# A two-layer graph network on one core: more of layer 0's gathers done as products, and the sums of a batch read later

## The chip, the cores and the metric

The kernel runs on one core of a Trainium2 chip. The metric is the device time in microseconds (us) of one execution; lower is better. Engines are named as in the profile: PE multiplies matrices (PEld loads its weights), DVE is the vector engine, ACT the scalar engine, POOL is GpSimd, SP issues DMAs.

## The reference

There are 12,500 nodes with 48 features and 200,000 edges, sorted by destination. Both layers take the features of each edge's source node, turn them into a message, add the messages up at the destination, and normalise.

```
# layer 0
tmp = concatenate([x[dst], x[src], edge_attr_32], axis=1)
h   = relu(tmp @ W1 + b1)
x1  = layernorm(x + segment_sum(h @ W2 + b2, dst))
# layer 1
m   = relu(x1[src] + edge_attr_48)
out = layernorm((1 + eps) * x1 + x1 + segment_sum(m, dst))
```

## The kernel before

The edges are cut into 391 groups of 512 (`NCHUNK`), each of 4 tiles of 128 edges. One group passes per step `k` of a loop; `run` (L620) calls a list of stages at each step, each with its own distance `d`, so that stage `f` works on group `k - d`. The order in which instructions are written is the order on every engine's queue. The function `lead0` comes last in each step of layer 0.

**Source features by gather.** `gather` (L247) issues one indirect DMA on POOL for one tile: 4 for a group. In layer 0 `fetch0` writes them into the tile `cat` six steps ahead (`AHEAD`). The pool of `cat` has 12 buffers; the last that reads a `cat` is `sum0`, at step g + 4. So the gather of group g waits until PE is through `sum0` of group g - 12, which happens at step g - 8. In layer 1 the tile is `xs`, also with 12 buffers, read by `message1` (`m`, L705).

**Source features by product.** Some groups are not gathered. Their features are made as one-hot matrices times the node table, two groups (8 tiles) to a batch (`products`, L530), as in these steps:

- `place` writes on DVE 8 small comparisons (`which_e`, L485), PE transposes them (L490) into the PSUM tile `which`; in layer 1 ACT makes a `copy` of it (L539).
- `edge_of` (L512) opens three PSUM tiles `ps` with multiplications by zeros; the same function closes them at the end.
- For each of the 98 blocks of 128 nodes (`NT`) a comparison on all 8 tiles gives a one-hot matrix `o` (`select`, L495, DVE; in layer 1 one block in five by `select_by_act`, L500 and L502, ACT), and `multiply` (L507) does 8 matmuls with the block `xp`. The matmuls of one step's blocks are written in the next step.
- `take` (L520) adds the three pieces of each sum on DVE (`made`, L523), one reduction for each of the tiles `ps`.

`products` is a generator; each step calls it once. In layer 0 a call does 2 and 3 blocks by turns (`BPS0 = (2, 3)`), so a batch lasts 40 steps and 8 batches serve the 16 groups 65, 85, ..., 365 (`FIRST0`, `EVERY0`, `NPE0`), from step 20 (`BEGIN0`) to 340. In layer 1 a call does 5 blocks (`BPS`), a batch lasts 20 steps, and 19 batches serve 38 groups: 20, 30, ..., 390. Six groups at the front of layer 1 (`FRONT`) are gathered from the table `front_dram`, with the last segment's rows added by products (`front`).

**Other work of a step in layer 0** on PE: `hidden0` (8 matmuls, L598), `sum0` (8, L613), `turn0` (4 transposes, L587), then the product matmuls. Every 28 groups a segment of nodes ends: `finish0` (`segment_sums`, layer norm, write of `x1_dram`) and, two steps later, `project` of a coming segment. From step `END0` on the finished table is loaded again, two steps for a segment, and split into `xp` for layer 1 (`split`).

**Layer 1** on PE: `sum1` (8 matmuls, L725) into a bank for 12 groups, opened and closed with zeros (L722, L730), then the product matmuls; on DVE `fill1` (`hot`, L695), `message1`, the comparisons; `drain1` and `finish1` at the end of a bank and of a segment. `some_products` calls the generator from group `BEGIN1` on.

Of the kernel before, what the change touches and what calls it, by code (L numbers as in the profile page):

```python
# [32 lines left out]
F32 = mybir.dt.float32  # L33
# [6 lines left out]
P = 128  # L40
# [3 lines left out]
D = 48  # L44
# [4 lines left out]
NT = -(-N // Q)  # L49
# [9 lines left out]
NSEG = NT // NB  # L59
# [10 lines left out]
FIRST = 20  # L70
EVERY = 10
NPE = 38
BEGIN1 = 4
BATCH = 2
BPS = 5
BY_ACT = 2
PIECES = 3

FIRST0 = 65
EVERY0 = 20  # L80
NPE0 = 16
BPS0 = (2, 3)
SPLIT0 = 2
BEGIN0 = 20
END0 = 341

PE_GROUPS0 = [FIRST0 + EVERY0 * i for i in range(NPE0)]
PE_GROUPS = [FIRST + EVERY * i for i in range(NPE)]
# [1 line left out]
assert PE_GROUPS[0] >= FRONT  # L90

assert PE_GROUPS[-1] < NCHUNK and PE_GROUPS0[-1] < NCHUNK
assert 2 * NT < BATCH * EVERY0 * sum(BPS0) and BEGIN0 > SPLIT0 + NSEG + 1
assert CHUNK * N % E == 0
assert NSEG * NB == NT
STEP = CHUNK * N // E
# [64 lines left out]
def windowed(ctx, tc, dram, flag, x, src, dst, e32, e48, w1, b1, w2, b2, eps, out):  # L161
# [15 lines left out]
    psum = layer0.enter_context(tc.tile_pool(name="psum0", bufs=1, space=bass.MemoryType.PSUM))  # L177
# [109 lines left out]
    for op, by, plus, to in (  # L287
# [5 lines left out]
            by, None, op0=op,  # L293
        )
        nc.vector.tensor_scalar(
            bits[:, FRONT + NPE :, :], src_g[:, FIRST0 : PE_GROUPS0[-1] + 1 : EVERY0, :],
            by, None, op0=op,
        )
        nc.vector.tensor_scalar(to, bits, plus, None, op0=ALU.add)
    begin.close()  # L300
    onehots = layer0.enter_context(tc.tile_pool(name="onehots0", bufs=2 * max(BPS0)))
    product = layer0.enter_context(tc.tile_pool(name="product0", bufs=1))
# [126 lines left out]
    def rows_of(table, s):  # L429
        return table[s * SN : (s + 1) * SN, :].rearrange("(t p) d -> p t d", p=Q)  # L430

    def split(t, s):
        for i in range(PIECES):
            piece = xp[:, s * NB : (s + 1) * NB, i, :]
            nc.scalar.activation(piece, t, AF.Copy)
            if i < PIECES - 1:
                rest = node.tile([Q, NB, D], F32, name="rest")
                nc.vector.tensor_tensor(rest, t, piece, op=ALU.subtract)
                t = rest

    def finish0(s):
# [6 lines left out]
        if s < NSEG - 1:  # L448
            nc.scalar.dma_start(rows_of(front_dram, s), x1)
        if last_group(s) >= END0:  # L450
            split(x1, s)
# [15 lines left out]
    def last_group(s):  # L467

        return max(g for g in range(NCHUNK) if low(g) < (s + 1) * SN)
# [7 lines left out]
    PER = 512 // (PIECES * D)  # L477

    def place(first, tiles, name, bufs):

        which = psum.tile([Q, tiles, P], BF16, name=name, bufs=bufs)
        which_e = product.tile([P, tiles, Q], BF16, name="which_e")
        for j in range(tiles):
            i = first + j // TPC
            nc.vector.tensor_scalar(  # L485
                which_e[:, j, :], iota_1, part[:, i, j % TPC : j % TPC + 1],
                block[:, i, j % TPC : j % TPC + 1], op0=ALU.is_equal, op1=ALU.mult,
            )
        for j in range(tiles):
            nc.tensor.transpose(which[:, j, :], which_e[:, j, :], ident16)  # L490
        return which

    def select(which, b):
        o = onehots.tile([Q, which.shape[1], P], BF16, name="o")
        nc.vector.tensor_scalar(o, which, float(b + 1), None, op0=ALU.is_equal)  # L495
        return o

    def select_by_act(copy, b):
        square = product.tile([Q, copy.shape[1], P], BF16, name="square")
        nc.scalar.activation(square, copy, AF.Square, bias=less[:, b : b + 1])  # L500
        o = onehots.tile([Q, copy.shape[1], P], BF16, name="o_act", bufs=2)
        nc.scalar.activation(o, square, AF.Relu, bias=1.0, scale=-1.0)  # L502
        return o

    def multiply(ps, o, b):
        for j in range(o.shape[1]):
            nc.tensor.matmul(  # L507
                ps[j // PER][:, j % PER, :], o[:, j, :], xp[:, b, :, :],
                start=False, stop=False, skip_group_check=True,
            )  # L510

    def edge_of(ps, start):  # L512
        for t in ps:
            n = t.shape[1] * PIECES * D
            nc.tensor.matmul(
                t.rearrange("p k c d -> p (k c d)"), zeros[:, :P], zeros[:, :n],
                start=start, stop=not start,
            )

    def take(ps, first, batch):  # L520
        xs = product.tile([P, batch * TPC, D], F32, name="made", bufs=FRONT // BATCH)
        for k, t in enumerate(ps):
            nc.vector.tensor_reduce(  # L523
                xs[:, k * PER : k * PER + t.shape[1], :], t.rearrange("p k c d -> p k d c"),
                AX.X, ALU.add,
            )
        for i in range(batch):
            made[ahead[first + i]] = xs[:, i * TPC : (i + 1) * TPC, :]

    def products(begin, count, batch, blocks, per_step, by_act, banks, bufs):  # L530


        tiles = batch * TPC
        for first in range(begin, begin + count, batch):
            which = place(first, tiles, banks[0], bufs)
            copy = None
            if by_act is not None:
                copy = product.tile([Q, tiles, P], BF16, name="copy", bufs=2)
                nc.scalar.activation(copy, which, AF.Copy)  # L539
            ps = [  # L540
                psum.tile([P, min(PER, tiles - k), PIECES, D], F32, name=banks[1 + k // PER],
                          bufs=bufs)
                for k in range(0, tiles, PER)
            ]
            edge_of(ps, True)
            last = []
            todo, step = list(blocks), 0
            while todo:
                n = per_step[step % len(per_step)]
                now = [  # L550
                    (b, select_by_act(copy, b) if i == by_act else select(which, b))
                    for i, b in enumerate(todo[:n])
                ]
                todo, step = todo[n:], step + 1
                for c, o in last:
                    multiply(ps, o, c)
                last = now
                yield
            for c, o in last:
                multiply(ps, o, c)  # L560
            edge_of(ps, False)
            take(ps, first, batch)


    cat, h, pt, ph, pa, hot = {}, {}, {}, {}, {}, {}
# [54 lines left out]
    def run(stages, adds, finish, lead):  # L620
# [13 lines left out]

    whole = {}
    work0 = products(
        FRONT + NPE, NPE0, BATCH, range(NT), BPS0, None, ("which", "sums0", "sums1", "sums2"), 1
    )

    def lead0(k):  # L640
# [10 lines left out]
        for s in range(NSEG):  # L651
# [3 lines left out]
            if k == SPLIT0 + s + 2:  # L655
                split(whole.pop(s), s)
            if last_group(s) < END0:
                if k == END0 + 2 * s + 1:
                    whole[s] = seg.tile([Q, NB, D], F32, name="whole", bufs=2)
                    nc.sync.dma_start(whole[s], rows_of(x1_dram, s))  # L660
                if k == END0 + 2 * s + 4:
                    split(whole.pop(s), s)
# [24 lines left out]
    psum = ctx.enter_context(tc.tile_pool(name="psum", bufs=1, space=bass.MemoryType.PSUM))  # L687
# [69 lines left out]
    banks = ("pm", "ph", "ph", "pm")  # L757

    def front():
# [19 lines left out]
        take(*before, BATCH)  # L779

    rest = products(FRONT, NPE, BATCH, range(NT), (BPS,), BY_ACT, banks, 2)

    def some_products(g):
        if g >= BEGIN1:
            next(rest, None)
# [225 lines left out]
```

## Time and profile before

| what | value |
|---|---|
| median of 3 runs | 3701.22 us (3698.91 to 3702.09) |
| the profiled execution, its own time | 3699.33 us |
| its span, first to last instruction | 3697.6 us |
| mean granted clock of PE | 0.885 |
| gathers in layer 0 / front / layer 1 | 1500 / 24 / 1388 |
| first gather; last of layer 0; last of all, ends at | 7.1; 1893.2; 3679.5 us |

Times in the text are from the start of the profiled span. In a line of the timeline the columns are start, duration over all of its instructions, engine, source line, operation, what it writes and reads, its shape, the count, and in brackets the idle time of the engine before it with what ended that. In a table by stretches each engine has its busy time and, in brackets, its instructions; the clock, the DMA share and GB/s follow.

### The profile page before, as it was taken

The numbers are of one execution on the slowest core, as the hardware profiler recorded it, in microseconds if no ns is written. First come the engines' busy times: TensorE is split into PE (matmuls) and PEld (weight loads), VectorE is DVE, ScalarE is ACT, GpSimd is POOL, SyncE is SP. The second block draws the span as 40 slices with busy tenths as digits, with TensorE's granted clock in tenths as the row PEclk, the third lists the DMA queues.
The fourth block names the chain that finished last, engine by engine and source line by source line (L and its number), as shares of the span: only waits on it lengthen the run. The fifth ranks groups of instructions, "written<-read, shape, count | busy, mean of one in ns | idle before, by whom it ended". The sixth has DMA issues, their size and how long they took to land. (4 is left out here: it accounts for less than half of the span.)

```text
span 3697.6 us, 87599 instructions
## 1 busy us (share of the span) xinstructions
PE 3348.4 (91%) x33806; PEld 2968.8 (80%) x33806; DVE 2683.3 (73%) x5415; ACT 1365.6 (37%) x2178; POOL 2774.8 (75%) x2923
## 2 busy tenths in 40 slices
PE   5888998998999899887889999999999999999996
PEld 4887988897888798886768887888888888888884
DVE  4765876676777686674438788788878888888883
ACT  2211211121112121113215555565556555655562
POOL 7777777777777777777776777777777777777776
PEclk8887988898989898897659999999999999999996
DMA  4222222122222212223211122122212221222121
GB/s 94 50 50 44 47 50 52 39 55 47 46 47 53 51 44 49 49 48 68 46 35 37 43 46 46 42 52 46 46 43 46 51 46 37 52 46 51 37 52 35
DMA packets 326421, 177.43 MB, mean 48 GB/s; under 512 B 144384, under 2 KB 325744, under 8 KB 326000
## 3 DMA queue, kind: packets, MB, share of 16 engines
q0 software_dynamic: 93184, 71.75, 11.3%
q1 hardware_dynamic: 203152, 88.86, 9.0%
q10 hardware_dynamic: 29664, 11.16, 1.1%
q8 instruction: 269, 4.41, 0.5%
q14 instruction: 152, 1.25, 0.1%
HBM read 156.51 MB, written 15.03 MB: 46 GB/s over the span
## 5 line engine op out<-in xcount | busy, mean ns | idle before, releaser
L247 POOL DMA_INDIRECT cat<-in_x_dram,src_i x1500 | 1429.2, 953 | 460.8 <-issue 310.3
L247 POOL DMA_INDIRECT xs<-x_dram,src_i x1388 | 1320.0, 951 | 435.9 <-issue 291.1
L507 PEld LDWEIGHTS <-o 128*128 128x128 bf16 x18296 | 1250.4, 102 | 99.4 <-DVE o L495 41.9
L495 DVE TENSOR_SCALAR o<-pm 128x1024 bf16<-128x1024 bf16 x1503 | 942.5, 686 | 62.2 <-ACT copy L539 27.1
L507 PE MATMUL ph<-xp,o 128*128 128x144 bf16 x8976 | 808.8, 231 | 0.0
L602 ACT ACTIVATE h<-ph 128x512 f32<-128x512 f32 x391 | 233.0, 596 | 1110.7 <-PE pa L613 1086.1
L598 PE MATMUL ph<-wcat,cat_t 128*128 128x128 f32 x3128 | 507.4, 313 | 106.4 <-ACT h L602 106.3
L598 PEld LDWEIGHTS ph<-wcat,cat_t 128*128 128x128 f32 x3128 | 448.0, 221 | 127.4 <-ACT h L602 120.8
L725 PE MATMUL pt<-hot,msg 128*48 128x128 f32 x3128 | 447.9, 290 | 56.5 <-ACT msg L711 56.5
L495 DVE TENSOR_SCALAR o<-which 128x1024 bf16<-128x1024 bf16 x784 | 495.3, 680 | 3.1 <-PE which L490 3.0
L507 PE MATMUL sums<-xp,o 128*128 128x144 bf16 x6272 | 488.6, 238 | 0.0
L725 PEld LDWEIGHTS pt<-hot,msg 128*48 128x48 f32 x3128 | 341.0, 129 | 141.4 <-ACT msg L711 63.8
L507 PE MATMUL pm<-xp,o 128*128 128x144 bf16 x2978 | 438.9, 230 | 0.0
L613 PE MATMUL pa<-cat,h 128*128 128x48 f32 x3128 | 431.6, 285 | 5.4 <-DVE pa L606 5.1
L613 PEld LDWEIGHTS pa<-cat,h 128*128 128x128 f32 x3128 | 429.2, 212 | 6.8 <-issue 4.7
L500 ACT ACTIVATE square<-copy,less 128x1024 bf16<-128x1024 bf16 x380 | 430.7, 1133 | 0.7
L502 ACT ACTIVATE o_act<-square 128x1024 bf16<-128x1024 bf16 x380 | 401.6, 1057 | 17.2 <-PE pm L507 5.8
L587 PE MATMUL pt<-ident,cat 128*128 128x128 f32 x1564 | 292.4, 302 | 82.5 <-DMA cat<-in_x_dram,src_i 79.3
L695 DVE TENSOR_TENSOR hot<-pa,rel 128x512 f32<-128x512 f32 x391 | 269.8, 690 | 97.6 <-PE pt L725 96.6
L591 DVE COPY cat_t<-pt 128x512 f32<-128x512 f32 x391 | 266.9, 683 | 72.3 <-PE pt L587 68.9
L711 ACT ACTIVATE msg<-m 128x192 f32<-128x192 f32 x391 | 141.5, 362 | 456.9 <-DVE m L705 408.4
L587 PEld LDWEIGHTS pt<-ident,cat 128*128 128x128 f32 x1564 | 214.7, 171 | 110.2 <-DMA cat<-in_x_dram,src_i 105.7
(118 smaller groups left out, 2412.1 us busy)
## 6 DMA issues: line engine op xcount, KB each, us to landing
e48c<-in_e_dram SPq DMA_DIRECT2D x78, 480.0 KB
e32c<-in_e_dram SPq DMA_DIRECT2D x78, 320.0 KB
cat<-in_x_dram,src_i POOLq DMA_INDIRECT x1500
xs<-x_dram,src_i POOLq DMA_INDIRECT x1388
wcat<-a SPq DMA_DIRECT2D x391, 24.0 KB
a<-a ACTq DMA_DIRECT2D x14, 256.0 KB
a<-a ACTq DMA_DIRECT2D x14, 192.0 KB
x_seg<-in_x_dram SPq DMA_DIRECT2D x14, 168.0 KB
```

The lines of the kernel that those rows point to most:

```text
L247: nc.gpsimd.indirect_dma_start(out=t, out_offset=None, in_=table, in_offset=bass.IndirectOffsetOnAxis(ap=src_i[:, g * TPC + j : g * TPC + ...
L495: nc.vector.tensor_scalar(o, which, float(b + 1), None, op0=ALU.is_equal)
L500: nc.scalar.activation(square, copy, AF.Square, bias=less[:, b : b + 1])
L502: nc.scalar.activation(o, square, AF.Relu, bias=1.0, scale=-1.0)
L507: nc.tensor.matmul(ps[j // PER][:, j % PER, :], o[:, j, :], xp[:, b, :, :], start=False, stop=False, skip_group_check=True,)
L587: nc.tensor.transpose(pt[g][:, j, :], cat[g][:, j, :], ident[:P, :P])
L591: nc.vector.tensor_copy(h[g], pt.pop(g))
L598: nc.tensor.matmul(ph[g][:, j, :], t[:, j, :], wcats[g % NW], start=True, stop=True)
L602: nc.scalar.activation(h[g], ph.pop(g), AF.Relu)
L613: nc.tensor.matmul(pa[g][:, 0, :], t[:, j, :], hot[:, j, :], start=j == 0, stop=j == TPC - 1)
L695: nc.vector.tensor_tensor(o, numbers[:, None, :].to_broadcast([P, TPC, W1]), rel1[:, g, :, None].to_broadcast([P, TPC, W1]), op=ALU.is_equal,)
L725: nc.tensor.matmul(bank[k][:, i * STEP : i * STEP + W1], msg[:, j, :], o[:, j, :], start=False, stop=False, skip_group_check=True,)
```

## The change

Layer 0 makes 20 groups by products instead of 16: 58, 75, ..., 381 (every 17th). A call does 3 blocks at every step, so a batch lasts 33 steps, and ten batches run from step 20 to 350. The splits for layer 1 begin at 352 instead of 341. In layer 1 the products begin one step later.

In `products`, for both layers, `take` of a batch is written later: no longer right after the matmuls that close its sums, but after the next batch's `place`, `copy` and first comparisons. The next batch's `ps` and their opening zeros follow `take`, since they use the same PSUM banks. The last batch's `take` comes at the end.

```diff
-BEGIN1 = 4
+BEGIN1 = 5
...
-FIRST0 = 65
-EVERY0 = 20
-NPE0 = 16
-BPS0 = (2, 3)
+FIRST0 = 58
+EVERY0 = 17
+NPE0 = 20
+BPS0 = (3,)
 SPLIT0 = 2
 BEGIN0 = 20
-END0 = 341
+END0 = 352
...
         tiles = batch * TPC
+        before = None
         for first in range(begin, begin + count, batch):
             which = place(first, tiles, banks[0], bufs)
             copy = None
             if by_act is not None:
                 copy = product.tile([Q, tiles, P], BF16, name="copy", bufs=2)
                 nc.scalar.activation(copy, which, AF.Copy)
-            ps = [
...
-            edge_of(ps, True)
-            last = []
+            ps = last = None
             todo, step = list(blocks), 0
             while todo:
...
                 todo, step = todo[n:], step + 1
-                for c, o in last:
-                    multiply(ps, o, c)
+                if ps is None:
+                    if before:
+                        take(*before)
+                    ps = [
+                        psum.tile([P, min(PER, tiles - k), PIECES, D], F32,
+                                  name=banks[1 + k // PER], bufs=bufs)
+                        for k in range(0, tiles, PER)
+                    ]
+                    edge_of(ps, True)
+                else:
+                    for c, o in last:
+                        multiply(ps, o, c)
                 last = now
                 yield
             for c, o in last:
                 multiply(ps, o, c)
             edge_of(ps, False)
-            take(ps, first, batch)
+            before = ps, first, batch
+        take(*before)
```

More of the change, by code (lines that the diff above doesn't have):

```diff
@@ L92 @@
 assert PE_GROUPS[-1] < NCHUNK and PE_GROUPS0[-1] < NCHUNK
-assert 2 * NT < BATCH * EVERY0 * sum(BPS0) and BEGIN0 > SPLIT0 + NSEG + 1
+assert NT < BATCH * EVERY0 * BPS0[0] and BEGIN0 > SPLIT0 + NSEG + 1
 assert CHUNK * N % E == 0
@@ L539, in products @@
                 nc.scalar.activation(copy, which, AF.Copy)
-            ps = [
[L541 to L544, printed above, removed]
-            edge_of(ps, True)
-            last = []
+            ps = last = None
             todo, step = list(blocks), 0
```

## The prediction

> **What bounds the kernel now.** I read the page first, then the lists of waits, then tables by stretches, then the timeline of single steps.
>
> ```profile
> L247 POOL DMA_INDIRECT cat<-in_x_dram,src_i x1500 | 1429.2, 953 | 460.8 <-issue 310.3
> L247 POOL DMA_INDIRECT xs<-x_dram,src_i x1388 | 1320.0, 951 | 435.9 <-issue 291.1
> ...
> POOL xs L247 <- DVE m L705: 22.3, 31, 13.2
> ...
> 371.00:434.00 63.00, 63.00 (x727) 62.80 (x726) 56.35 (x119) 14.58 (x37) 47.76 (x51) 1.00 0.20 44
> ```
>
> POOL is busy 75%, yet it never rests: each gather takes 0.95 us and is followed by 0.30 us of its own issue. From 7.1 us to the end of the last gather there is one other gap over 0.4 us: 13.2 us at 1953.6, where the twelve `xs` buffers are full and wait for the first `m` of layer 1. So the end is 2912 gathers plus that gap plus about 18 us of drain. In layer 0 one gather costs (1893.5 - 7.1) / 1500 = 1.258 us, a group 5.03.
>
> The last line (PE, PEld and DVE stand first) says why that isn't all: for 63 us PE has no gap. Comparing, group by group, the start of the transposes (L587, or L725 in layer 1) with the end of its gather gives PE's **lag**. In layer 0 it swings between 0 and 31.6 us (group 66); a gather waits for `sum0` twelve groups back, so POOL stops at a lag of about 7 x 5.0 = 35 us, 30 with a product group between. The closest approach was 1.8 us, at group 73. In layer 1 the lag is 45.5 us at group 12 and falls to 7.4 at 378: PE is a little faster than POOL.
>
> What a step costs PE:
>
> ```profile
> 919.53 0.62 PE L587 MATMUL pt<-ident,cat 128*128 128x128 f32 x4
> 919.99 1.66 PE L507 MATMUL sums<-xp,o 128*128 128x144 bf16 x24
> ...
> 923.25 0.62 PE L587 MATMUL pt<-ident,cat 128*128 128x128 f32 x4
> 923.71 1.16 PE L507 MATMUL sums<-xp,o 128*128 128x144 bf16 x16
> ...
> 926.48 0.62 PE L587 MATMUL pt<-ident,cat 128*128 128x128 f32 x4
> ```
>
> From turn to turn, 3.72 us with three blocks (24 matmuls) and 3.23 with two: 2.22 + 0.50 per block. A boundary of batches in layer 1:
>
> ```profile
> 2301.85 1.71 PE L515 MATMUL ph<-zeros 1*128 1x432 f32 x4
> 2303.40 0.64 PE L515 MATMUL pm<-zeros 1*128 1x288 f32 x2
> 2304.88 2.08 PE L490 MATMUL pm<-ident,which_e 128*128 128x128 bf16 x8 [0.84 <-DVE which_e L485]
> 2306.89 3.24 PE L515 MATMUL ph<-zeros 1*128 1x432 f32 x4
> 2309.93 1.16 PE L515 MATMUL pm<-zeros 1*128 1x288 f32 x2
> ...
> 2302.87 1.33 DVE L523 TENSOR_REDUCE made<-ph 128x144 f32<-128x432 f32 x2 [5.18 <-PE ph L515]
> 2304.12 0.45 DVE L523 TENSOR_REDUCE made<-pm 128x96 f32<-128x288 f32 x1
> 2304.49 2.13 DVE L485 TENSOR_SCALAR which_e<-iota,part,block 128x128 bf16<-128x128 f32 x8
> 2308.05 2.49 DVE L495 TENSOR_SCALAR o<-pm 128x1024 bf16<-128x1024 bf16 x4 [1.44 <-ACT copy L539]
> ```
>
> DVE waits 5.2 us to read the sums, then makes `which_e`, then PE transposes at DVE's pace. The next `sum1` starts at 2311.03, 9.2 us after the closing zeros began.
>
> **What the Trainium skill says.** "TensorE: Matmul & The Clock Gate", Part 1: PE's clock halves after an idle window of about 3.4 us and returns after a busy one. The trace agrees: the same zeros start every 0.39 us when closing and every 0.76 when opening. "PSUM — Partial Sum Buffer", on bank collisions: two engines must not use one bank at once, reads included; so DVE's comparisons wait for ACT's `copy` (27.1 us over 19 batches, 1.4 each). "Perfetto Trace Analysis", on the tensor engine's instruction: ACT, DVE and GpSimd are strictly in order, and PE only pulls weight loads ahead; so opening zeros that wait hold all of PE behind them.
>
> **Part 1: 16 gathers fewer.** 16 x 1.258 = 20.1 us off POOL, all on the path, if PE keeps up.
>
> **Part 2: PE's load in layer 0.** A batch before: 40 steps x 2.22 + 98 blocks x 0.50 + the boundary. That costs 17.9 us for the two steps at group 180, where 5.9 is usual: 12.0 extra. `finish0` and `project` add 30.2 - 10.7 = 19.5 us in three steps (groups 146 to 148), once in 28 steps: 0.70 a step. Before: (88.8 + 49 + 12) / 40 + 0.70 = 4.45 us a step, against 19/20 x 5.03 = 4.78 that POOL leaves. After: (73.3 + 49 + 12) / 33 + 0.70 = 4.77, against 16/17 x 5.03 = 4.73. PE goes from 93% to 101% of what POOL grants. DVE gains half a comparison (0.31 us) a step: 56.35/18.1 + 0.31 = 3.4 us in a step of 3.72, hidden.
>
> Over 330 steps 0.04 x 330 = 13 us of lag builds up, and each cluster of boundary, finish and project adds up to 32 us at once. I kept an account of the lag step by step: from 13 us at group 20, add the step's cost, take off 5.01 for each gathered group, stop POOL at the limit. For the kernel before it gives peaks of 33 and 26 where the trace has 31.6 and 24.5, and no stop. For the changed one it stops POOL near groups 262 and 290, 8.2 us in all. As the account ran 1 to 2 us high, I take **7**. It is steep: 1 us less for each boundary gives 5.6, 1 us more 17, 0.05 us more for each step 21. The end is safe: after step 350 a step costs 2.7, so the lag is gone before group 390 in spite of the product group 381; splits up to step 378 (ACT 3 x 0.48 us, DVE 2 x 0.51) and four more product groups' ACT copies (0.35 each) run in idle time.
>
> **Part 3: the boundary.** From the start of the closing zeros, layer 1, after: `which_e` is long made (DVE is free 4 us earlier). Zeros to 2.1; transposes at PE's own pace 0.6, to 2.75; `copy` to 3.85; four comparisons at 0.62, to 6.35; the first reduction to 7.0. Only then can the first bank be opened: PE stands 4.2 us, goes cold, and the zeros take 4.1, to 11.1 instead of 9.2: **+1.9 us**. The stall by `take` goes from DVE, and PE's opening zeros are late in its place; behind them stand `sum1` and all matmuls. In layer 0 there is no copy, three comparisons and a wait of 2.6 us: opening ends at 9.5 instead of 9.2, or at 7.5 if the clock stays up: 0 taken, -1.7 to +0.3.
>
> **Part 4: layer 1.** With one step fewer ahead of the first `m`, four comparisons (2.4 us, 1963.2 to 1965.6) leave the 13.2 us gap: -2.4. PE loses 18 x 1.9 = 34 us over the 18 boundaries and has one loaded step more (2 us), so its lag at 378 is 43 instead of 7. `xs` stops POOL only near 61. Behind the last batch a step costs PE about 1.5 us (1.9 and 1.7 in the trace, with a cold start): 12 x 1.5 = 18. POOL's part from the gather of 378 to the last sum is 54.4 us (3629.1 to 3683.5). PE would end 43 + 18 - 54 = 7 us later; the last sums then run warm (2.1 us instead of 3.65), so **+5**. Bounds: 0 if the boundary grows by 1.5 us or less, +27 (stalls included) at 3 us.
>
> **Sum**: -20.1 + 7 - 2.4 + 5 = -10.5 us. Against the profiled execution's 3699.3 (span 3697.6 and 1.7 around it) 3688.8; the median stands 1.9 above that execution: **3690.7**.
>
> **Rivals.** (A) PE keeps up everywhere: boundaries get no longer, and coinciding events hide each other; for it speaks that four steps with both kinds of event took 48.4 us (groups 258 to 261) where the account has 50.4; against it the opening zeros that wait for `take`. Then -22.5: 3678.7. (B) Slower: PE becomes layer 0's bound. One mechanism: the mean step grows beyond 3.72 because DVE, at 92% in a three-block step, holds PE up. From 0.05 us a step on POOL's stops eat the gain (21 us); at 0.1 they are 37, so -20.1 + 37 - 2.4 + 5 = +19.5: 3721. Against it: PE, not DVE, ends each three-block step now, with DVE waiting 0.3 us. A layer-1 boundary of +3 us would end near there too (+12). (C) Moving `take` is idle in effect, as PE still has the sums, transposes and zeros in one row: then part 4 costs nothing and part 2 stands: -15.5, 3685.7.
>
> **Numbers.** A measurement of this kernel can tell about 0.2% (7.4 us) from no change. My case 0.54, of which 0.38 below that line and 0.16 within it; A and C 0.22, faster; B and its like 0.18; 0.06 for a near balance of gain and stops. Faster 0.60, same 0.22, slower 0.18. The range runs from A (3679) to a mild B (3709).
>
> **What would show it.** 1484 `cat` gathers; POOL's row with gaps over 1 us around groups 250 to 320 of layer 0, 4 to 14 us in all; three-block steps of 3.72; the gap at the start of layer 1 near 10.8; PE's wait at L515 of about 4 us, from DVE L523, at 18 boundaries; DVE's wait at L523 gone; a lag near 40 at group 378 and sums L725 without waits at the end. A lag at 378 below 20 refutes part 3, three-block steps above 3.8 speak for B, and a layer 0 without POOL gaps refutes part 2.

## The result, and the profile after

The changed kernel takes 3718.49 us (median of 5 runs, 3713.53 to 3725.63) against 3699.67 us (3698.39 to 3702.09) for the kernel before: a ratio of 1.0051, 95% interval 1.0037 to 1.0066. It is slower by 18.8 us; 3690.7 was predicted. The profiled execution took 3725.63 us, span 3723.9: 26.3 us more than the span before, and the slowest of the five. From `turn0` on, line numbers are 7 higher than before (L594 `turn0`, L605 `hidden0`, L609 `h`, L620 `sum0`, L732 `sum1`, L712 `m`); `copy` is at L541 (539 before).

From the page of the changed kernel: the chain that ended last by engine, then two of the costliest groups. (The page of the kernel before follows its chain for less than 1% of the span, so the two chains can't be compared.)

```profile
PE 81%; DVE 6%; DMA 4%; issue 3%; POOL 2%; ACT 2%; ACTq 0%; DVEq 0%; SPq 0%; POOLq 0%
...
L247 POOL DMA_INDIRECT cat<-in_x_dram,src_i x1484 | 1409.6, 950 | 493.8 <-issue 302.0
...
L495 DVE TENSOR_SCALAR o<-pm 128x1024 bf16<-128x1024 bf16 x1503 | 944.5, 683 | 157.2 <-ACT copy L541 97.1
```

There are 16 gathers fewer, each as long as before (950 ns), yet POOL's idle time in front of them has grown from 460.8 to 493.8 us. The list of waits says for what (line waited in, what ended the wait, us in total, times, longest). POOL, changed kernel:

```profile
POOL cat L247 <- ACT h L609: 44.6, 30, 10.6
...
POOL xs L247 <- DVE m L712: 21.9, 27, 14.0
```

POOL, kernel before:

```profile
POOL cat L247 <- ACT h L602: 10.1, 33, 0.3
```

A wait of 0.3 us is the usual distance between two gathers, with whatever happened to end last put beside it. The longest is now 10.6 us: POOL is stopped, 14 times in layer 0, 37.9 us in all beyond those 0.3. The event named, `h`, lies just ahead of `sum0`, the last reader of the twelve `cat` buffers. Laid beside PE's matmuls, 12 of the 14 stops end 0.77 us after the last matmul of a `sum0`, 12 or 13 groups back (the others 0.10 and 1.08 us). So POOL waits for PE: PE has become the bound of layer 0. The table by stretches (us; PE, PEld, DVE, ACT, POOL with their instructions; clock, DMA share, GB/s) has, for the stretch shown of before:

```profile
371.00:434.00 63.00, 63.00 (x748) 62.81 (x746) 57.00 (x118) 13.56 (x35) 47.76 (x51) 1.00 0.20 44
```

PE is as full in this stretch as it was. What differs is that PE no longer catches up: before, its lag came back to zero again and again and PE waited for gathers there (the 1.8 us of the prediction is how near POOL came to a stop, not a lag); now, from group 92 to group 350, the lag never falls below 7.9 us and PE never waits for a gather.

Where the 26.3 us of span lie:

| part | predicted | profiled execution |
|---|---|---|
| 16 gathers off POOL (16 x 1.258) | -20.1 | -20.1 |
| POOL stopped in layer 0 | +7 | +37.9 |
| pitch of the other gathers of layer 0 | 0 | -4.5 |
| gap at the start of layer 1 (13.2 to 14.0) | -2.4 | +0.8 |
| gathers of layer 1 | 0 | +2.2 |
| from the last gather to the end (18.1 to 28.1) | +5 | +10.0 |

### The profile page after: what moved, and what is told of

It reads as the page before. It is cut to its first block, busy times and chain, and to the rows that moved or that the text cites. A ratio compares the mean times of both kernels' runs of the same rounds, so it can differ in the third digit from the quotient of the medians.

```text
span 3723.9 us, 90966 instructions
## 1 busy us (share of the span) xinstructions
PE 3381.5 (91%) x35414; PEld 3034.4 (81%) x35414; DVE 2803.2 (75%) x5633; ACT 1365.7 (37%) x2182; POOL 2757.4 (74%) x2907
## 3 DMA queue, kind: packets, MB, share of 16 engines
q0 software_dynamic: 92672, 71.36, 11.1%
## 4 chain that ended last, share of the span: by engine, by line
PE 81%; DVE 6%; DMA 4%; issue 3%; POOL 2%; ACT 2%; ACTq 0%; DVEq 0%; SPq 0%; POOLq 0%
PE ph L507 20%; PE sums L507 12%; PE pt L732 11%; PE ph L605 10%; PE pa L620 8%; PE pm L507 6%; PE pt L594 4%; PE ph L515 3%; DMA cat<-in_x_dram,src_i 3%; POOL cat L247 2%; PE sums L515 2%; DVE o L495 2%; PE px L329 1%; PE pt L737 1%; PE pt L729 1%
## 5 line engine op out<-in xcount | busy, mean ns | idle before, releaser
L247 POOL DMA_INDIRECT cat<-in_x_dram,src_i x1484 | 1409.6, 950 | 493.8 <-issue 302.0
L507 PEld LDWEIGHTS <-o 128*128 128x128 bf16 x19864 | 1345.4, 101 | 103.8 <-DVE o L495 40.5
L495 DVE TENSOR_SCALAR o<-which 128x1024 bf16<-128x1024 bf16 x980 | 614.1, 680 | 63.3 <-PE which L490 58.0
L609 ACT ACTIVATE h<-ph 128x512 f32<-128x512 f32 x391 | 232.9, 596 | 1123.4 <-PE pa L620 1095.2
L605 PE MATMUL ph<-wcat,cat_t 128*128 128x128 f32 x3128 | 491.3, 306 | 108.6 <-ACT h L609 108.4
L507 PE MATMUL sums<-xp,o 128*128 128x144 bf16 x7840 | 587.2, 235 | 0.0
L605 PEld LDWEIGHTS ph<-wcat,cat_t 128*128 128x128 f32 x3128 | 431.5, 214 | 131.1 <-ACT h L609 123.3
L732 PE MATMUL pt<-hot,msg 128*48 128x128 f32 x3128 | 437.6, 285 | 32.0 <-ACT msg L718 31.8
L620 PE MATMUL pa<-cat,h 128*128 128x48 f32 x3128 | 427.5, 284 | 6.9 <-DVE pa L613 6.9
L620 PEld LDWEIGHTS pa<-cat,h 128*128 128x128 f32 x3128 | 423.4, 210 | 9.2 <-PE ph L605 4.3
L732 PEld LDWEIGHTS pt<-hot,msg 128*48 128x48 f32 x3128 | 334.0, 126 | 113.6 <-ACT msg L718 36.2
L594 PE MATMUL pt<-ident,cat 128*128 128x128 f32 x1564 | 270.0, 296 | 18.7 <-DMA cat<-in_x_dram,src_i 15.7
L387 DVE TENSOR_TENSOR agg<-agg,pa 128x96 f32 x391 | 99.2, 254 | 195.9 <-PE pa L620 194.3
```

The source lines that it names most:

```text
L247: nc.gpsimd.indirect_dma_start(out=t, out_offset=None, in_=table, in_offset=bass.IndirectOffsetOnAxis(ap=src_i[:, g * TPC + j : g * TPC + ...
L507: nc.tensor.matmul(ps[j // PER][:, j % PER, :], o[:, j, :], xp[:, b, :, :], start=False, stop=False, skip_group_check=True,)
L594: nc.tensor.transpose(pt[g][:, j, :], cat[g][:, j, :], ident[:P, :P])
L605: nc.tensor.matmul(ph[g][:, j, :], t[:, j, :], wcats[g % NW], start=True, stop=True)
L609: nc.scalar.activation(h[g], ph.pop(g), AF.Relu)
L620: nc.tensor.matmul(pa[g][:, 0, :], t[:, j, :], hot[:, j, :], start=j == 0, stop=j == TPC - 1)
```

## The experiments

The change has three edits: more groups, sums read late, and layer 1's first batch begun one step later. The question was which of them turns -10.5 into +18.8. Many of the kernels ran on chips where the kernel before itself takes 5472 to 5535 us, because PE stands still there for no reason that the profile shows (last section; called the late kind here); each ratio is against the kernel before on the same chip, and the numbers on stops and steps are from the chips where it takes 3700.

### One edit at a time

`groups_only` is the kernel before with the constants of layer 0 alone, its sums read early as before:

```diff
-FIRST0 = 65
-EVERY0 = 20
-NPE0 = 16
-BPS0 = (2, 3)
+FIRST0 = 58
+EVERY0 = 17
+NPE0 = 20
+BPS0 = (3,)
...
-END0 = 341
+END0 = 352
```

`late_only` is the kernel before with the new `products` alone: 16 groups, `BEGIN1` 4. `groups_late0` is `groups_only` with the new `products` in layer 0 alone; it stands there as `products_late`, and layer 1 keeps the old function:

```diff
-    work0 = products(
+    work0 = products_late(
```

`open_first` is the changed kernel with `take` and the opening zeros moved ahead of the first comparisons; the next batch's `place` and `copy` stay ahead of `take`:

```diff
                 nc.scalar.activation(copy, which, AF.Copy)
-            ps = last = None
+            if before:
+                take(*before)
+            ps = [
...
+            edge_of(ps, True)
+            last = []
...
-                if ps is None:
-                    if before:
-                        take(*before)
...
-                else:
-                    for c, o in last:
-                        multiply(ps, o, c)
+                for c, o in last:
+                    multiply(ps, o, c)
```

Expected on the first chip:

> The 20 groups with three blocks a step in layer 0, and nothing else: sums read right behind the matmuls as before, layer 1 untouched. Theory L (the later reading makes each boundary of batches longer for PE, in layer 0 by 1.3 us and a clock window, in layer 1 by 1.9): boundaries in layer 0 back at 12 us extra, POOL's stops in layer 0 8 us or less (38 in the changed kernel), layer 1 as before with its 13 us gap; 20.1 - 8 = 12 us faster than before: 3688. Theory G (the groups themselves overload PE in layer 0, the reading order is innocent): stops near 38 us as in the changed kernel, layer 0 ends 13 us later than before, 3713.

> Only the later reading of the sums, in both layers, with 16 groups in layer 0 and the first products of layer 1 where they were. Theory L: layer 0 has slack enough (PE 93% of what POOL leaves), no or few stops (under 5 us); in layer 1 each of 18 boundaries 13.7 instead of 11.8 us, lag near 43 at group 378, last sum some 10 us after what POOL allows: 3709 to 3712. Theory G: layer 1 ends as before, 3700.

> The 20 groups, and the later reading in layer 0 only; layer 1 as before. Theory L: stops of about 38 us in layer 0 as in the changed kernel, layer 1 without overrun: 13 us later than before at the end of layer 0 and at the end, 3711 to 3714; slower than the groups alone by 25. Theory G: the same time as the groups alone, to 3 us.

> The changed kernel, with the reading of the sums and the opening zeros moved ahead of the next batch's first comparisons; the small comparisons, transposes and the copy stay ahead of it. Theory L (what costs is that the opening zeros wait for the comparisons): opening follows the transposes at once, the wait of 2.6 and 4.2 us is gone and the clock stays up more often; boundary step in layer 1 about 7.5 to 9.5 us instead of 13.7, lag at group 378 below 10, stops in layer 0 under 5 us, gap of layer 1 near 11: 20 us faster than before, 3680. Rival (the later reading itself costs, wherever the zeros stand; or the clock falls all the same): boundary 11.8 or more, 3695 or more.

Expected on the second:

> The 20 groups with three blocks a step, sums read as before, layer 1 untouched, again, since on the first chip even the kernel before took 5473 us. Where the kernel before takes its 3700: theory L (the later reading lengthens each boundary of batches on PE): boundaries in layer 0 cost 12 us extra, POOL's stops there 8 us or less (38 in the changed kernel), layer 1 as before: 12 us faster than before, 3688. Theory G (the groups themselves overload PE): stops near 38 us, 3713.

> Only the later reading, in both layers, again. Theory L: under 5 us of stops in layer 0; in layer 1 boundaries of 13.7 us for 11.8, lag near 43 at group 378, 9 to 12 us slower than before: 3709 to 3712. Theory G: as before, 3700.

> The 20 groups, and the later reading in layer 0 only, again. Theory L: stops of about 38 us in layer 0, no overrun in layer 1: 3711 to 3714. Theory G: the time of the groups alone to 3 us.

> The changed kernel with the reading of the sums and the opening zeros ahead of the next batch's first comparisons, again. Theory L: boundary step in layer 1 of 7.5 to 9.5 us for 13.7, lag at group 378 below 10, stops in layer 0 under 5 us: 20 us faster than before, 3680. Rival (the clock falls all the same, or reading late costs wherever the zeros stand): boundary 11.8 or more, 3695 or more.

| kernel | where before takes 5472.9 us (e) | where it takes 3701.3 us (f) |
|---|---|---|
| groups_only | 1.0051 [1.0028, 1.0073] | 3699.08, 0.9991 [0.9983, 1.0000] |
| late_only | 1.0044 [1.0029, 1.0059] | 3705.01, 1.0004 [0.9996, 1.0012] |
| groups_late0 | 1.0082 [1.0063, 1.0102] | 3705.68, 1.0013 [1.0006, 1.0020] |
| open_first | 0.9997 [0.9984, 1.0010] | 3677.41, 0.9934 [0.9921, 0.9948] |

No single edit makes the loss, and neither theory holds whole. The groups alone bring nothing that can be told apart: 20 us of gathers less, 22.0 us of stops more (theory L had 8 or less, theory G 38). The late reading of layer 0 costs another 6.6 us by medians (3705.68 - 3699.08). Of the 13.0 us between these two profiled executions 8.5 are stops and 2.5 the gap at the start of layer 1 (16.3 us for 13.8).

On 16 groups the late reading brings no stop at all: PE still has room there. `late_only` was to lose 9 to 12 us by an overrun of PE behind the last gather, and lost 3.7 by medians, which the interval can't tell from nothing. Its trace has no such overrun (lag 32.0 us at group 378, 17.8 us from the last gather to the end); it is 5.5 us of span longer because the gap at the start of layer 1 is 20.6 us for 13.2. In that gap PE makes the products of the six front groups, in code that no edit touches, and the granted clock differs: the three rows of opening zeros take 4.2, 2.3 and 2.2 us in the kernel before, 4.2, 4.2 and 4.2 in `late_only`, and about 4.2, 4.2 and 2.2 in `groups_late0`, after_begin4 (below) and the changed kernel.

To see that the stops are PE's time and nothing else, I added up PE's steps, from `turn0` to `turn0`, over groups 88 to 349, in the account of the prediction (262 steps of 3.72, seven boundaries of 11.6 extra, ten ends of a segment of 19.5) and in five traces; `after_begin4` follows below and has the same layer 0 as the changed kernel.

| | PE's time for 262 steps, us | a step | stops in layer 0, us |
|---|---|---|---|
| account of the prediction | 1250.8 | 4.77 | 8.2 (7 taken) |
| groups_only | 1266.2 | 4.83 | 22.0 |
| after_begin4 | 1269.0 | 4.84 | 26.6 |
| groups_late0 | 1275.1 | 4.87 | 30.5 |
| changed kernel | 1279.8 | 4.88 | 37.9 |

Every us that PE takes more comes back as about one us of stop. groups_late0, after_begin4 and the changed kernel have the same code in layer 0 and still lie 11 us apart.

In open_first the stops are gone, and its time is the one theory L gave (3677.41 us, 3680 expected). POOL there:

```profile
POOL cat L247 <- ACT h L607: 7.9, 26, 0.3
```

A boundary of layer 0 in it, PE in the timeline:

```profile
923.47 2.20 PE L515 MATMUL sums<-zeros 1*128 1x432 f32 x6
925.60 0.62 PE L490 MATMUL which<-ident,which_e 128*128 128x128 bf16 x8
926.15 2.20 PE L515 MATMUL sums<-zeros 1*128 1x432 f32 x6
928.28 1.71 PE L603 MATMUL ph<-wcat,cat_t 128*128 128x128 f32 x8
```

and DVE:

```profile
924.50 1.70 DVE L523 TENSOR_REDUCE made<-sums 128x144 f32<-128x432 f32 x3 [2.64 <-PE sums L515]
926.26 1.89 DVE L495 TENSOR_SCALAR o<-which 128x1024 bf16<-128x1024 bf16 x3
```

DVE reads the sums while PE still closes and transposes, so the opening zeros follow without a wait, at full clock: 2.20 us. From the start of the closing zeros to `hidden0` 4.8 us pass. In the changed kernel, PE:

```profile
934.29 2.20 PE L515 MATMUL sums<-zeros 1*128 1x432 f32 x6
936.42 0.62 PE L490 MATMUL which<-ident,which_e 128*128 128x128 bf16 x8
939.63 4.17 PE L515 MATMUL sums<-zeros 1*128 1x432 f32 x6 [2.58 <-DVE made L523]
943.73 2.07 PE L605 MATMUL ph<-wcat,cat_t 128*128 128x128 f32 x8
945.60 1.78 PE L620 MATMUL pa<-cat,h 128*128 128x48 f32 x8
947.18 1.08 PE L594 MATMUL pt<-ident,cat 128*128 128x128 f32 x4
948.05 3.02 PE L507 MATMUL sums<-xp,o 128*128 128x144 bf16 x24
```

DVE:

```profile
937.08 1.89 DVE L495 TENSOR_SCALAR o<-which 128x1024 bf16<-128x1024 bf16 x3 [4.43 <-PE which L490]
938.89 1.48 DVE L523 TENSOR_REDUCE made<-sums 128x144 f32<-128x432 f32 x3
```

Three comparisons stand on DVE's queue ahead of `made`; PE waits 2.58 us for them, the opening zeros run at half the clock, and 9.4 us pass. The row of 24 matmuls at 948.05 is still slow (3.02 us; 1.66 is usual): the clock stays low until 950.9.

The wait is not what makes the clock fall. In the changed kernel it falls at 937.22, 0.2 us after the wait has begun. In open_first it falls too, at 928.71, although PE has had no gap since 922; behind PE lie 4.8 us of zeros and transposes. There the opening zeros are done by then, and the clock is back at 935.53. The low spell lasts 6.8 us in place of 13.7. So the rival's "the clock falls all the same" was right, and its 3695 us was not.

Over nine boundaries the 4.6 us between the two orders come to 41 us of PE, more than the 37.9 us of stops. In layer 1 the overrun goes the same way: 19.2 us from the last gather to the end, for 28.1. The boundary steps there take 7.4 to 13.3 us, 10.1 on the mean (7.5 to 9.5 expected).

### How many groups PE can carry

`groups18` asks whether the 22 us of groups_only are a mean that is a little too high or clusters of events that come whatever the mean. It is groups_only with

```diff
-FIRST0 = 58
-EVERY0 = 17
-NPE0 = 20
-BPS0 = (3,)
+FIRST0 = 62
+EVERY0 = 19
+NPE0 = 18
+BPS0 = (2, 3, 3)
```

> 18 groups in layer 0 (every 19th, 2, 3 and 3 blocks by turns), sums read as before, layer 1 as before. PE's demand is (37 x 2.22 + 49 + 12) / 37 + 0.70 = 4.57 us a step against 18/19 x 5.03 = 4.76: 96%. Theory (the knee is at 100%, and the 22 us of stops with 20 groups come from standing at 101 to 102%): under 3 us of stops, 10 us faster than before, 3690. Rival (clusters of events stop POOL at any load): 5 or more us of stops, 3696 or more.

> 18 groups in layer 0 (every 19th, 2, 3 and 3 blocks by turns), sums read as before, layer 1 as before; again. PE's demand 4.57 us a step against 4.76 that POOL leaves, 96%. Theory K (the knee is at 100%): under 3 us of stops, 10 us faster than before, 3690. Rival (clusters of events stop POOL at any load): 5 or more us of stops, 3696 or more.

> Products for 18 groups in layer 0, sums read early as before, nothing else changed. Ten of the twenty us that 20 groups free on POOL. If the stops with 20 groups (22 us) come from a step that is 0.05 us too long on the mean, the room of half as much again as the step gives back ends nearly all stops: under 5 us of stops, 3691 to 3695 us. If they come in clusters around cold spells of PE whatever the mean, 10 us and more of stops stay: 3698 to 3702 us.

On two chips of the late kind no change can be told: 0.9998 [0.9983, 1.0013] and 1.0002 [0.9986, 1.0018]. On the other (before 3701.82) it takes **3691.46 us, 0.9973 [0.9962, 0.9984]**. There is not one stop in layer 0, and the 10.4 us gained are the 8 gathers (8 x 1.258 = 10.1). With 19 groups between products POOL leaves 18/19 x 5.03 = 4.77 us a step; PE's cost, worked out as in the prediction with the 37 steps that a batch lasts, is (37 x 2.22 + 49 + 12) / 37 + 0.70 = 4.57. Between groups 90 and 345 its trace has eight places where the lag is back near zero and PE waits for gathers. Clusters of events still raise the lag, to 29.5 us at group 318, but they start from there and don't reach the limit: the mean decides.

### Where layer 1 begins

`after_begin4` is the changed kernel with one constant put back:

```diff
-BEGIN1 = 5
+BEGIN1 = 4
```

> The changed kernel with the products of layer 1 begun a step earlier, as before. In the late-only run the lag at group 378 was 32 us and there was no overrun, in the changed kernel 45 and 10 us. Theory S (starting a step later moves boundaries onto ends of segments and adds a step): lag near 33 here, overrun under 3, 5 to 10 us faster than the changed kernel, 3708 to 3714. Theory 0 (the start makes no difference; the late-only run had the small lag because its front part ran slowly): lag 43 to 45, 3718.

> The changed kernel with the products of layer 1 begun a step earlier, as before; again, for a chip on which the kernel before takes 3700. Theory S (starting a step later moves boundaries onto ends of segments and adds a step): lag at group 378 near 33 instead of 45, overrun under 3 us, 5 to 10 us faster than the changed kernel, 3708 to 3714. Theory 0 (the start makes no difference): lag 43 to 45, 3718.

> The changed kernel, with layer 1's first rank begun one step earlier (BEGIN1 4 as in the kernel before, in place of 5), where the kernel before takes about 3700 us. If the overrun of PE beyond the last gathers (10 us more than before) comes from where the banks' and segments' ends fall together, it changes by that: 3708 to 3714 us. If it comes from the 1.9 us a boundary that PE loses in layer 1, it stays: 3715 to 3722 us.

1.0124 [1.0098, 1.0149] and 1.0131 [1.0097, 1.0164] on the late kind of chip; on the other 3710.63 us (3699.95 to 3721.02), 1.0022 [1.0013, 1.0031]. That is about 8 us under the changed kernel, and the intervals of the two ratios do not meet, though they come from two comparisons. From the last gather to the end it takes 22.3 us in place of 28.1; the lag at group 378 is 40.8 in place of 45.0. Between groups 12 and 378 PE takes 1651.2 us in place of 1659.1. Most of that lies at six boundaries (groups 59, 119, ..., 359) that the changed kernel has right ahead of the end of a bank: over six steps there it takes 0.7 to 1.8 us more, 7.5 in all. The changed kernel also has two boundaries of 17.4 and 17.2 us (groups 39 and 99), where the boundary and the end of a segment fall into one step, for 13.7 to 14.1 with `BEGIN1` 4; over six steps these cost no more than 1.2 and 0.9 us, since the segment's end is then missing from the step behind. In return the gap at the start of layer 1 is 16.3 us in place of 14.0, the 2.4 us of the prediction. The time lies in the range of the first view, but only 3.5 us of the difference (5.8 at the end less 2.3 at the start) are accounted for so in the traces. The rest lies in layer 0, where the two are the same code and the profiled runs differ by 11 us of stops; it isn't settled how much of it is chance.

### Opening first, with fewer and with more products

`open_first16` is open_first with the 16 groups of before (and `BEGIN1` 4). It ran on a late kind of chip alone:

> The kernel before (16 groups, 2 and 3 blocks by turns, start of layer 1 as before) with the order that opens before the first comparisons. Theory P (POOL sets the end as long as PE keeps up): the shorter boundaries buy nothing by themselves, no stops before and none now: 3696 to 3702. Rival (PE's time counts directly): 15 us or more faster, 3685.

0.9866 [0.9841, 0.9890], against 0.9997 for 20 groups in that order on another chip of this kind. The rival was right here: where PE bounds both layers, the shorter boundary is gain by itself, and the four groups seem to cost more than they save, as groups_only does there (1.0051). open_first16 was not run where the kernel before takes 3700 us.

`open_first_42` is open_first with a product every 9 groups of layer 1:

```diff
-EVERY = 10
-NPE = 38
+EVERY = 9
+NPE = 42
...
-BPS = 5
+BPS = 6
```

(and ten buffers instead of eight for the one-hot matrices).

> The order that opens first with 20 groups, and in layer 1 42 groups by products instead of 38 (every 9th, six blocks a step, ten buffers for the one-hot matrices). 16 gathers fewer: 20 us, if PE keeps up. By the sums so far a batch costs PE 17 x 4.1 + 1.1 + some 10 for boundary, banks and ends of segments, 81 us for 18 groups, against 16 x 5.02 = 80 from POOL: balanced, with 45 us of lag to fill. Theory: 15 to 20 us faster than the 3677 of the order alone, 3657 to 3662. Rival (six blocks tie DVE and PE together, a step takes 4.5): lag over 60, stops in layer 1, 3677 or more.

> The order that opens first with 20 groups, and in layer 1 42 groups by products instead of 38 (every 9th, six blocks a step, ten buffers for the one-hot matrices); again. PE needs 81 us for 18 groups, POOL 80: balanced, with 45 us of lag to fill. Theory: 15 to 20 us faster than the 3677 of the order alone, 3657 to 3662. Rival (six blocks tie DVE and PE together, a step takes 4.5): lag over 60, stops in layer 1, 3677 or more.

> The kernel that opens the next sums ahead of the first comparisons (3677 us), with products in layer 1 for 42 groups of the batch in place of what it has (EVERY 9, six a time). It takes gathers off POOL in layer 1 and gives PE more in each step. If PE has room left in layer 1, 3665 to 3674 us; if PE is already layer 1's bound there, the gathers stop and it is 3678 to 3690 us.

1.0093 [1.0072, 1.0114] and 1.0048 [1.0030, 1.0066] on the late kind; on the other 3745.24 us, 1.0117 [1.0102, 1.0133], 68 us slower than open_first and far above both ranges of the last expectation. POOL waits:

```profile
POOL xs L247 <- DVE m L710: 108.5, 43, 15.3
```

The longest, 15.3 us, is the gap at the start of layer 1, which open_first has with 14.7; the stops behind it are new. `m` stands on DVE's queue behind `hot` (L700), which waits for `sum1` of PE (45.8 us between 2000 and 3600). PE is busy for 1575 of these 1600 us. A step with six blocks takes PE 4.11 us, 3.61 with five, not the 4.5 by which DVE was to hold it, and a batch lasts 17 steps in place of 20: layer 1 crosses the same line as layer 0 did, from PE just ahead of POOL to just behind.

## Why the prediction was wrong, step by step

**Part 1 was right**: 1484 gathers at the same price.

**Part 2 is where it failed: a term of the sum was mis-sized.** The mechanism, PE at about 101% of what POOL grants and POOL stopped, was named; so was its steepness ("0.05 us more for each step 21"). The account's mean was 4.77 us a step; the trace of groups_only has 4.83, and with it 22.0 us of stops, not 7. (The changed kernel has 4.88 and 37.9; its stops begin at group 101, where they were foreseen near 262 and 290, and the longest is at 326.) The 15.4 us of PE over 262 steps split up as follows:

| | account | measured in groups_only | extra |
|---|---|---|---|
| plain step, 211 of them | 3.72 | 3.72 | 0.5 |
| two steps at a boundary, six clear of 118 to 120 | 19.0 | 19.0 to 20.2, mean 19.6 | 3.1 |
| three steps of a segment's end, nine | 30.7 | 30.9 to 31.7, mean 31.3 | 6.1 |
| the step two ahead of that end, nine | 3.72 | 4.11 | 3.5 |
| groups 118 to 120, both together | 42.3 | 44.5 | 2.2 |

No line is off by more than 11%; each fell on the same side. Each term had been read from one instance, and from a low one: the two steps at group 180 take 17.9 us in the kernel before, those at 100 and 300 18.1 and 19.2; the three steps from 146 on take 30.4 (30.2 was read), those of the other segments 30.3 and more. The step two ahead of a segment's end was left out, though the kernel before shows it, with 4.06 us for 3.22 at groups 88, 144 and 228. An account that is 1.2% low is nothing where PE has 7% of room, as before, and decides everything where it has none. The check against the kernel before could hardly show it: there POOL sets the pace and PE's waits absorb such errors. Nor did the account run high there throughout, which was the ground for taking 7: the next highest lags of that trace are 28.0 us (group 149) and 27.5 (262), not 24.5. Groups 118 to 120 also contradict the hint that events which coincide save time; with the stops, Rival A falls.

**Rival B gave the right size by the wrong cause.** It had PE as layer 0's bound and 3721 us, but by a three-block step held up by DVE. That its figure is near 3718.49 is luck: the step stayed at 3.72.

```profile
956.40 0.62 PE L594 MATMUL pt<-ident,cat 128*128 128x128 f32 x4
956.86 1.66 PE L507 MATMUL sums<-xp,o 128*128 128x144 bf16 x24
...
960.12 0.62 PE L594 MATMUL pt<-ident,cat 128*128 128x128 f32 x4
```

**Part 3, layer 1, was right.** A boundary of layer 1 in the changed kernel, PE:

```profile
2327.58 1.71 PE L515 MATMUL ph<-zeros 1*128 1x432 f32 x4
...
2329.71 0.93 PE L490 MATMUL pm<-ident,which_e 128*128 128x128 bf16 x8
2334.88 3.21 PE L515 MATMUL ph<-zeros 1*128 1x432 f32 x4 [4.24 <-DVE made L523]
...
2338.99 1.94 PE L732 MATMUL pt<-hot,msg 128*48 128x128 f32 x8
```

DVE:

```profile
2331.74 2.48 DVE L495 TENSOR_SCALAR o<-pm 128x1024 bf16<-128x1024 bf16 x4 [6.26 <-ACT copy L541]
2334.14 1.11 DVE L523 TENSOR_REDUCE made<-ph 128x144 f32<-128x432 f32 x2
```

The transposes run at PE's own pace, DVE waits for `copy`, four comparisons stand ahead of `made`, and PE stands 4.24 us (4.2 predicted). From the start of the closing zeros to `sum1` 11.4 us pass (11.1 predicted). The step over a boundary takes 13.7 us for 11.8: +1.9, as predicted. DVE's wait at L523 for layer 1 has shrunk from 96.4 us to 7.3 and PE has one in its place, 4.2 us at each of 18 boundaries, so Rival C falls:

```profile
PE ph L515 <- DVE made L523: 76.3, 18, 4.2
PE sums L515 <- DVE made L523: 23.3, 9, 2.6
```

**Part 3, layer 0, was taken at nothing and cost 6.6 us** between the medians of groups_only and groups_late0. The opening ends at 9.4 us, as worked out (9.5). What was left out is what comes behind it: the clock comes back later, so the next step's matmuls run slow. The Trainium skill, "TensorE: Matmul & The Clock Gate", Part 1, has the clock back after one busy window of about 3.4 us; here PE is without a gap from 939.63 and is slow until 950.9, 11.3 us. The same part has the clock fall after an idle window, which the prediction took up; in open_first it fell at 928.71 with PE never idle. The measurement decides. Which rows count as busy isn't shown here: the zeros may not. A boundary's price has to be read to the first step at the old speed, not to the end of the opening. Over the seven boundaries between groups 88 and 349 the three traces with this code spend 2.8, 6.8 and 9.9 us more on the two steps than groups_only, 0.4 to 1.4 each, where -1.7 to +0.3 was given; a part of the 6.6 us is the longer gap at the start of layer 1.

**Part 4 had the mechanism, and its sizes a little low.** The lag at group 378 is 45.0 us (43 predicted), and the 12 sums behind it take PE 20.5 us (18): 4.5 of the 5 us by which the overrun was underrated. That `BEGIN1` 5 puts six boundaries right ahead of the end of a bank was not seen (7.5 us of PE). The 34 us that PE was to lose over the boundaries are not firm: between groups 12 and 378 late_only loses 24.2 to the kernel before, after_begin4 with the same layer 1 31.8. The 2.4 us of the gap were there between two kernels that differ in `BEGIN1` alone, but the kernels that read sums late and begin at 4 had a gap of 16.3 us (groups_late0, after_begin4) or 20.6 (late_only) where the kernel before has 13.2. The longer gaps lie in the rows of the front groups at the low clock, as shown above; why the clock falls there in these kernels isn't settled.

By medians, each against its own kernel before: groups -2.2 (predicted -13), late reading in layer 0 +6.6 (0), late reading in layer 1 +4.4 and its later begin +10.0 (together +2.6), in all +18.8. The last two are differences between comparisons on different chips, and the traces account for only a part of them: of the profiled execution's miss which is 36.8 us, the stops in layer 0 are 30.9.

## What to carry to other kernels

Where an engine that fills gaps comes near 100% of what the bounding engine grants, an account good to 1% is too coarse to tell gain from loss: give the size before the knee too (18 groups won 0.27%, 20 nothing), and price each kind of event by all of its instances in the trace, not by one. Look at the pacing too: a batch of the changed kernel lasts 33 steps but serves 34 groups, so PE makes its sums a little earlier than they are needed. Spread over 34 steps the account gives (34 x 2.22 + 49 + 12) / 34 + 0.70 = 4.71 us, an estimate from the prediction's numbers; no run tried it. Moving a wait is not removing it: put what frees a buffer ahead of the work that only follows in the queue. Here reading the sums ahead of the comparisons, with the next batch's placing still ahead of both, takes 3677.41 us, 0.9934 [0.9921, 0.9948] of the kernel before, and is the best version found.

## What the runs showed of the hardware

- **The same layer 0 lost 26.6, 30.5 and 37.9 us in three traces.** The plain steps are 3.72 us in all of them; boundaries and ends of segments differ with where the low spells of the clock fall. That a kernel bound by PE scatters more from run to run isn't shown: on one chip groups_late0 spread over 10.3 us (21 runs) and the kernel before over 11.8 (41 runs), though after_begin4 spread over 21 (18 runs) on another.
- **The clock can fall while PE has work.** In open_first it fell at 928.71 us, with PE busy without a gap from 922 to 940, behind 4.8 us of multiplications by zeros and transposes, and it was low for 6.8 us. Whether the zeros, the transposes or both fail to hold it was not tried.
- **Chips on which PE stands still without a reason in the profile.** There the kernel before takes 5472 to 5535 us. PE's list of waits for groups_only on one of them has

```profile
PEld L507 <- issue: 874.5, 1345, 2.0
```

  where the same kernel has 26.3 us in that line (137 times) on the other chip; the granted clock is lower too, 0.775 for 0.897. Gathers (953 ns) and comparisons (684 ns) last as long as elsewhere. POOL waits 728 us in layer 0 and 1031 in layer 1 for buffers that PE's work frees, so PE bounds both layers there and the same edits rank otherwise: 20 groups alone lose 0.5%, and 16 groups with the opening first gain 1.3%. What holds PE up was not found.
